# Two MoE stages of a graph network: weight pieces and slots ahead of a branch, two tiles mixed by products, and a shared expert's weights in another ring

## The chip, the cores and the metric

One core of a Trainium2 chip runs the whole kernel. The metric is the device time of one execution in microseconds (us); the time before is the median of three runs. One more execution was taken by the profiler: TensorE (PE) does the matmuls, PEld its weight loads, DVE is VectorE, ACT ScalarE, POOL GpSimd and SP SyncE, whose queue issues the weight transfers. Times in the text are us from the start of the profiled span.

## The reference

256 tokens of width 768 pass through four rounds; each round is a graph layer (gnn) and a feed-forward layer (ffn), with layer norms between, and every ffn adds its output to x. The change concerns the ffn of rounds 1 and 2, both a mixture of eight experts (MoE) of which each token takes two. Cut to what matters, with `x` the normed tokens:

```
# round 1 (layer 1)
logits = x @ Wr.T;  vals, idx = top_k(logits, 2);  weights = softmax(vals)
h = gelu(x @ Wi[e].T + bi[e]);  expert_out[e] = h @ Wo[e].T + bo[e]
out[t] = sum over the token's 2 experts of weights * expert_out[e][t]

# round 2 (layer 2)
w, idx = gate(x)                       # softmax scores, best 2 of 4 groups, best 2 experts
g = swiglu((x @ W1[e] + B1[e]) * (x @ W3[e] + B3[e]));  per_expert[e] = g @ W2[e] + B2[e]
out[t] = sum over 2 experts of w * per_expert[e][t]  +  shared_ffn(x)
shared_ffn(x) = swiglu((x @ Ws1 + Bs1) * (x @ Ws3 + Bs3)) @ Ws2 + Bs2
```

The kernel must be right for any routing; for the input timed here no expert gets more tokens than its tiles hold.

## The kernel before, in words

**Tiles of tokens.** Experts are ranked by their number of tokens (`ranked`, DVE; `who[r]` is the expert of rank r, L1021). Fixed tiles of 128 rows are given to ranks: `TILES1` has seven tiles (rank 0 has one and a half, ranks 1 to 4 one each, 5, 6 and 7 half ones), `TILES2` six. `dispatch` (L1024) works out for each token the two rows it has among all tiles (`places`) and a flag `over`, whether some expert overflows its tiles. If it does, a body under `tc.If(count > 0)` (L1439 and L1667) computes extra tiles; for this input it is jumped over. Every engine reads the flag and takes the branch for itself, and on the way around the body the engines step through semaphores so that all agree on the counts. `find` makes `slots`, the token of each tile row: DVE compares a count with `places` (`hot`, L1099), PE multiplies it with token numbers (L1104), DVE copies the result (L1107).

**A tile's work.** The first tile's rows in layer 1 are picked by products (`first_rows`, L1144). For the other tiles POOL gathers rows from a table in DRAM by indirect DMA (`take_rows`, L1120), PE transposes them (L1128), and PE multiplies: `up` (L1153, after a bias product at L1421 or L1641), then an activation (ACT, and DVE in layer 2), transposes of the result (L1202), and `finish`, the products ps_y with the second weights (L1153 too), ACT's copy to `y` (L1161) and ACT's DMA of `y` into `ys` in DRAM (L1210). The loop over tiles is staggered: up(u), then the transposes and ps_y of tile u - 1.

**Weights.** A piece is 1152 KB. `stream` keeps a list of pieces with their rings; `pump` issues each next one on SP as long as its ring has a free buffer, and `done` frees buffers in program order. Layer 1 has 16 pieces (wi and wo of eight ranks) in the ring "w" (`wpool`, RING = 8 buffers). In layer 2 the w_e pieces go there too, with four of the buffers held at first by the shared expert's up weights (s0 to s3), while w_down pieces and the shared expert's Ws2 go through the ring "d" of three. SP reads `who` into a register to form a piece's address (L1214), then issues the DMA (L87).

**The end of a layer.** Weights of the mix come from `rest` (L1058). It also makes, for the last tile, a mix matrix (`mix`, called neg in the profile, L1071 and L1073; transposed at L1076 and copied by ACT at L1078 to `mixT`), so that this tile's rows never go through DRAM: `end_tiles` multiplies `mixT` with its `y` (L1176) into the accumulators of each half of the tokens, which in layer 1 begin with the bias bo (L1478) and in layer 2 with the shared expert's products (`down_t`, L1114 and L1116). All other rows come back by `add_rows`: four indirect gathers yg from `ys` on POOL (L1120), each multiplied and added to x on DVE (L1169). Then DVE adds the accumulator (`add_acc`, L1370), norms (L150 to L160), and PE's transposes (L171) begin the next stage. Rows of `ys` that are asked for with a weight of zero were zeroed in the first stage.

**Order around the change.** Instructions marked `pin` keep program order on PE; a scheduler places the rest by its own cost estimates. In layer 1 the order before is: `dispatch`, `first_rows`, branch, first `pump`, `find`, softmax, loop. In layer 2: `up_shared(0)` (shared expert, L102), `dispatch`, `up_shared(1)`, branch, `pump`, `find`, first gather, `up_shared(2)`, `rest`, loop.

Of the kernel before, what the change touches and what calls it, by code (L numbers as in the profile page):

```python
# [13 lines left out]
OP = mybir.AluOpType  # L14
# [4 lines left out]
P = 128  # L19
# [34 lines left out]
def graph_ffn_stack_kernel(ctx: ExitStack, tc: tile.TileContext, a: dict, out: bass.AP):  # L54
# [969 lines left out]
    def dispatch(pool, plan_t, mask, before, total, is_r):  # L1024
# [32 lines left out]

        def rest(cw, last):  # L1058


            weights = tmp([P, NC, 2], "row_w")
            for i, t in enumerate((lo, hi)):
                nc.vector.tensor_tensor(t, t, ends[:, :, i, None].to_broadcast([P, NC, 8]), OP.is_equal)
                nc.vector.tensor_tensor(t, t, cw, OP.mult)
                nc.vector.tensor_reduce(weights[:, :, i], t, AX.X, OP.add)
            rel = tmp([P, NC, 2], "row_rel")
            nc.vector.tensor_scalar(rel, places, float(last * P), None, op0=OP.subtract)
            mix = neg1.rearrange("p c (j n) -> p c j n", j=2)
            for c in range(NC):
                for j in range(2):  # L1070
                    nc.vector.tensor_scalar(mix[:, c, j, :], count_up[:, :P], rel[:, c, j:j + 1], weights[:, c, j:j + 1],  # L1071
                                            op0=OP.is_equal, op1=OP.mult)
            nc.vector.tensor_tensor(mix[:, :, 0, :], mix[:, :, 0, :], mix[:, :, 1, :], OP.add)  # L1073
            ps = bank("ps_mix")[:, :N]
            for c in range(NC):
                nc.tensor.transpose(ps[:, c * P:(c + 1) * P], mix[:, c, 0, :], ident)  # L1076
            mixT = cnt1[:, 0, :]
            nc.scalar.copy(mixT, ps)  # L1078
            kept = tmp([P, NC, 2], "row_kept")
            nc.vector.tensor_scalar(kept, rel, 0.0, None, op0=OP.is_lt)  # L1080
            nc.vector.scalar_tensor_tensor(kept, rel, float(P), kept, op0=OP.is_ge, op1=OP.add)
# [81 lines left out]
    def add_rows(gathered, ys, rows, weights):  # L1163
        table = ys.rearrange("u p d -> (u p) d")
        for c in range(NC):
            for j in range(2):
                y = gathered("yg")
                take_rows(y, table, rows[:, c, j:j + 1])
                nc.vector.scalar_tensor_tensor(x[:, c, :], y, weights[:, c, j:j + 1], x[:, c, :], op0=OP.mult, op1=OP.add)  # L1169

    def end_tiles(accs, y, mixT):

        xn = normed()
        for c in range(NC):
            for i in range(2):
                pin(nc.tensor.matmul(accs[c][:, i, :384], mixT[:, c * P:(c + 1) * P], y[:, i * 384:(i + 1) * 384],  # L1176
                                     start=False, stop=True))
            add_acc(accs[c], c)
            norm(x, xn, D, c)
        return xn  # L1180
# [35 lines left out]
    def stream(pieces, held_by_others):  # L1216


        loaded, freed, rings, at = {}, set(), {"w": [None] * (RING - len(held_by_others)) + held_by_others}, [0]
        freed.add(None)  # L1220

        def pump():
            while at[0] < len(pieces):
                key, ring, bufs, load = pieces[at[0]]
                keys = rings.setdefault(ring, [])
                if len(keys) >= bufs and keys[len(keys) - bufs] not in freed:
                    return
                loaded[key] = load()
                keys.append(key)
                at[0] += 1  # L1230

        def done(*keys):
            freed.update(keys)
            pump()

        return loaded, pump, done

    TILES1 = [[(0, 0, 128)], [(0, 128, 64), (7, 0, 64)], *[[(r, 0, 128)] for r in range(1, 5)], [(5, 0, 64), (6, 0, 64)]]
    TILES2 = [[(0, 0, 128)], [(0, 128, 64), (7, 0, 64)], [(1, 0, 128)], [(3, 0, 64), (4, 0, 64)], [(2, 0, 128)],
              [(5, 0, 64), (6, 0, 64)]]  # L1240
    plans = [moe.tile([P, 3, 8], F32, name=f"plan{i}") for i in range(2)]
    results = [held.tile([len(t) + len(plan(t)[3]), P, D], F32, name=f"ys{i}") for i, t in enumerate((TILES1, TILES2))]
# [7 lines left out]
    def constants(pool):  # L1250
        zero = pool.tile([P, D], F32, name="zero")
        nc.gpsimd.memset(zero, 0.0)
        for i, tiles in enumerate((TILES1, TILES2)):
            more = results[i][len(tiles) - 1:]
            nc.gpsimd.dma_start(more.rearrange("u p d -> p u d"), zero[:, None, :].to_broadcast([P, more.shape[0], D]))
            for j, values in enumerate(plan(tiles)[:3]):
                for r, value in enumerate(values):
                    if r == 0 or value != values[r - 1]:
                        nc.gpsimd.memset(plans[i][:, j, r:], float(value))
# [123 lines left out]
    with tc.tile_pool(name="f1", bufs=1) as f1, tc.tile_pool(name="f1a", bufs=2) as f1a:  # L1383
# [10 lines left out]

        def load(r, kind):
            if kind == "wi":
                index[r] = nth(who, r)
            return load_piece(wpool, a["L1_ffn_WiT" if kind == "wi" else "L1_ffn_WoT"][index[r]], kind)

        index = {}  # L1400
        loaded, pump, done = stream([((r, kind), "w", RING, lambda r=r, kind=kind: load(r, kind)) for parts in TILES1
                                     for kind in ("wi", "wo") for r, first, _ in parts if first == 0], [])
        places, is_e, over, rest = dispatch(f1, plans[0], mask, before, total, is_r)
        more = plan(TILES1)[3]
# [31 lines left out]

        xgT = first_rows(f1, places, "first_xgT")
        count = nc.values_load(over[0:1, 0:1], min_val=0, max_val=1, **UNCHECKED)
        with tc.If(count > 0, preferred_fallthrough_block=False):  # L1439
            slots = find(f1, places, len(TILES1) * P, len(more), "slots1_more")  # L1440
            for j, r in enumerate(more):
                parts = [(r, 0, P)]
                for kind in ("wi", "wo"):
                    loaded[r, kind] = load(r, kind)
                g = up(tile_t(f1a, take(slots[:, j:j + 1]), "xgT"), parts, pick(f1a, is_e, parts))
                finish(f1a, ys[len(TILES1) + j], turned(f1a, g), views(parts, "wo"), parts)
            index.clear()
        pump()
        slots = find(f1, places, P, len(TILES1) - 1, "slots1")
        softmax8(cw)  # L1450
# [5 lines left out]
        for u, parts in enumerate(TILES1):  # L1456
            now = xgT
            if u < end:
                xg = take(slots[:, u:u + 1])
            if u == 0:  # L1460
                rows1, w1s, mixT = rest(cw, end)
            g = up(now, parts, pick(f1a, is_e, parts))
            free(u, "wi")
            if last is not None:
                gT = turned(f1a, last)
            if u < end:
                xgT = tile_t(f1a, xg, "xgT")
            if last is not None:
                finish(f1a, ys[u - 1], gT, views(TILES1[u - 1], "wo"), TILES1[u - 1])
                free(u - 1, "wo")  # L1470
            last = g
        add_rows(gathered, ys, rows1, w1s)
        gT = turned(f1a, last)
        accs = []
        for c in range(NC):
            accs.append(acc2("moe_acc"))
            for i in range(2):
                pin(nc.tensor.matmul(accs[c][:, i, :384], cwT[:, c * P:(c + 1) * P], bo[:, i * 384:(i + 1) * 384],  # L1478
                                     start=True, stop=False))
        xn = end_tiles(accs, finish(f1a, None, gT, views(parts, "wo"), parts), mixT)  # L1480

# [52 lines left out]
    with tc.tile_pool(name="f2", bufs=1) as f2, tc.tile_pool(name="f2a", bufs=2) as f2a:  # L1534
# [50 lines left out]
        before, total, is_r, who = ranked(f2, mask)  # L1585
        places, is_e, over, rest = dispatch(f2, plans[1], mask, before, total, is_r)
        index = {}

        def load(r, kind, ring=None):

            if r == "s":
                return load_piece(f2a, a["L2_ffn_Ws2"], "w_down", "down", DOWN)
            if r not in index:
# [97 lines left out]
        rows2, w2s, mixT = rest(cw, end)  # L1691
        cwT = weights_t(f2, cw, 9, "cwT2")
        xgT = tile_t(f2a, xg, "xgT")
        last = None
        for u, parts in enumerate(TILES2):
            own, now = pick(f2a, is_e, parts), xgT
            if u < end:
                xg = take(slots[:, u + 1:u + 2])
            acc = acc2("up1_acc")
# [21 lines left out]
        xn = end_tiles(accs, finish(f2a, None, gT, views(parts, "2"), parts), mixT)  # L1721

# [196 lines left out]
```

## Time and profile before

| what | us |
|---|---|
| median of 3 runs (1452.01 to 1456.68) | 1454.04 |
| the profiled execution | 1456.74 |
| its span in the profile | 1455.0 |
| layer 1's MoE, from the first L1144 product to the next stage's transposes (852.1 to 957.6) | 105.5 |
| layer 2's MoE, from its up_shared(1) to the next stage's transposes (1076.4 to 1257.9) | 181.5 |

The mean granted clock of TensorE over the span is 0.916. The profiled execution is 2.70 us above the median, so a sum made on its rows stands on a time that is that much longer. In the views of groups and waits, "idle before" is the time in which an engine had nothing to do ahead of an instruction, with what released it behind the arrow; a row of the timeline gives the start, the duration, the engine and line, and the tiles written and read. A window's row gives each engine's busy time, the granted clock, the share of the DMA engines and GB/s. Issue and landing of single DMAs, quoted in the text, are from the trace's instruction rows.

### The profile page before, as it was taken

How to read it: one execution, taken by the hardware profiler on the slowest of the kernel's cores; microseconds unless marked ns; L12 is line 12 of the kernel's file. 1: busy time of each engine (PE TensorE's matmuls, PEld its weight loads, DVE VectorE, ACT ScalarE, POOL GpSimd, SP SyncE). 2: the span in 40 equal slices, each digit the busy share in tenths (PEclk: the TensorE clock that was granted, in tenths of full speed). 3: DMA queues.
4: the chain of work that ended last, by engine and by line, in shares of the span. 5: the costliest groups of instructions: out<-in, count | busy, mean ns of one | idle time of the engine just before them, and what ended most of it. 6: DMA issues, size and time to landing. Idle time of an engine off the chain costs nothing. (4 is left out here: it accounts for less than half of the span.)

```text
span 1455.0 us, 13968 instructions
## 1 busy us (share of the span) xinstructions
PE 1259.4 (87%) x5081; PEld 775.6 (53%) x5102; DVE 670.2 (46%) x1273; ACT 477.0 (33%) x825; POOL 356.3 (24%) x194
## 2 busy tenths in 40 slices
PE   7999999789997874998989859866889999777998
PEld 4576444347643432854545445435576554466854
DVE  4421999930099996164352530067351011455023
ACT  1013877611287662241231122215221111163122
POOL 1001999800099991000203010111001000100000
PEclk9999999989999995999999969987989999775989
DMA  9323250215230023223732149922018998600000
GB/s 332 130 94 102 59 160 6 98 33 195 101 95 0 3 95 115 89 111 143 259 116 76 66 171 389 335 89 73 22 72 342 364 383 334 264 1 33 33 0 22
DMA packets 77689, 196.74 MB, mean 135 GB/s; under 512 B 9036, under 2 KB 23952, under 8 KB 77488
## 3 DMA queue, kind: packets, MB, share of 16 engines
q1 hardware_dynamic: 69088, 162.28, 31.2%
q0 software_dynamic: 6352, 28.33, 5.5%
q10 hardware_dynamic: 2176, 5.18, 1.0%
q8 instruction: 43, 0.70, 0.2%
q14 instruction: 30, 0.25, 0.1%
HBM read 177.45 MB, written 14.87 MB: 132 GB/s over the span
## 5 line engine op out<-in xcount | busy, mean ns | idle before, releaser
L784 POOL TENSOR_TENSOR gate<-gate,qT 128x2048 f32<-128x2048 f32 x64 | 287.8, 4535 | 242.4 <-ACT gate L764 242.0
L769 DVE TENSOR_REDUCE qiT<-gate 128x32 f32<-128x2048 f32 x96 | 215.0, 2279 | 16.2 <-POOL gate L784 15.2
L764 ACT ACTIVATE gate<-gate_acc,bg 128x1024 f32<-128x1024 f32 x192 | 209.8, 1114 | 38.1 <-PE gate_acc L760 35.5
L759 PE MATMUL gate_acc<-sela,ga 128*128 128x512 bf16 x363 | 139.2, 384 | 25.3 <-ACT gate L764 24.8
L760 PE MATMUL gate_acc<-selb,gb 112*128 112x512 bf16 x384 | 147.8, 385 | 1.2
L1153 PE MATMUL up_acc<-w_e,xgT 128*64 128x384 f32 (+1 forms) x432 | 96.4, 489 | 0.0
L760 PEld LDWEIGHTS <-gb 112*128 112x128 bf16 x384 | 37.6, 98 | 96.4 <-issue 71.5
L791 DVE TENSOR_TENSOR gate<-gate,ps_qy 128x2048 f32<-128x2048 f32 x32 | 72.9, 2278 | 0.2 <-ACT gate L764 0.2
L1153 PEld LDWEIGHTS up_acc<-w_e,xgT 128*64 128x64 f32 (+1 forms) x432 | 46.9, 154 | 44.7 <-issue 27.3
L759 PEld LDWEIGHTS <-ga 128*128 128x128 bf16 x384 | 37.8, 98 | 47.8 <-issue 2.2
L642 PE MATMUL ps_alpha<-w_qb,qiT 128*128 128x384 f32 x96 | 44.1, 553 | 19.8 <-DVE qiT L769 19.8
L566 DVE TENSOR_TENSOR ps_hg<-ps_hg,hg 128x384 f32<-128x384 f32 x8 | 4.5, 563 | 107.9 <-ACT hg L565 107.9
L326 PE MATMUL ps_pt<-ident,gat_z 128*128 128x128 f32 x104 | 23.8, 366 | 33.6 <-DVE gat_s L318 33.5
L1120 POOL DMA_INDIRECT yg<-ys,rows x8 | 7.6, 953 | 177.3 <-DMA w_a<-in_L_ffn_AT 118.6
L171 PE MATMUL ps_tr<-ident,xn 128*128 128x128 f32 x84 | 17.7, 380 | 35.4 <-DVE xn L160 20.3
L267 DVE CUSTOM_DVE_ANT_0 gat_dot<-xl,row 128x128 f32<-128x128 f32 (+2 forms) x56 | 23.8, 425 | 52.8 <-ACT xl L1520 19.6
L457 PE MATMUL ps_z<-w_rel,xT 128*128 128x384 f32 x144 | 47.9, 486 | 0.0
L457 PE MATMUL ps_z<-w_rel,nT 128*128 128x384 f32 x144 | 47.7, 491 | 0.0
L461 ACT COPY z<-ps_z 128x384 f32<-128x384 f32 x24 | 11.5, 479 | 105.0 <-PE ps_z L457 105.0
L1651 DVE TENSOR_TENSOR h<-up_acc,h 128x768 f32<-128x768 f32 x6 | 5.7, 958 | 80.1 <-PE up_acc L1153 80.1
L627 PE MATMUL ps_alpha<-w_qa,gT 128*128 128x384 f32 x96 | 40.1, 499 | 0.0
L338 PE MATMUL gat_acc<-xl,gat_pt 128*128 128x128 f32 (+2 forms) x128 | 34.9, 431 | 5.3 <-DVE gat_s L347 5.3
(444 smaller groups left out, 2192.7 us busy)
## 6 DMA issues: line engine op xcount, KB each, us to landing
w_e<-in_L_ffn_W SPq DMA_DIRECT2D x32, 1152.0 KB, 12.2
w_rel<-in_L_gnn_W_rel SPq DMA_DIRECT2D x12, 1152.0 KB, 8.3
wi<-in_L_ffn_WiT SPq DMA_DIRECT2D x8, 1152.0 KB, 15.0
wo<-in_L_ffn_WoT SPq DMA_DIRECT2D x8, 1152.0 KB, 15.5
w_down<-in_L_ffn_W SPq DMA_DIRECT2D x8, 1152.0 KB, 12.2
w_root<-in_L_gnn_W_root SPq DMA_DIRECT2D x4, 1152.0 KB, 11.1
w_ga<-in_L_gnn_WgAT SPq DMA_DIRECT2D x4, 1152.0 KB, 6.4
w_qa<-in_L_gnn_WqAT SPq DMA_DIRECT2D x4, 1152.0 KB, 5.7
```

Of the source, the lines that this page charges most:

```text
L267: pin(nc.vector.tensor_tensor_reduce(t, xl[:, c, h * C:(h + 1) * C], r[:, h * C:(h + 1) * C], 1.0, 0.0, OP.mult, OP.add, accum_out=a2[:, w ...
L338: pin(nc.tensor.matmul(accs[d][:, i, at:at + wide], pts[h, d][:, j, s, :], xl[:, s, lo:lo + wide], start=s == 0, stop=s == NC - 1))
L457: mm = nc.tensor.matmul(ps, hT[:, k, c * P:(c + 1) * P], w(k, i * 384, (i + 1) * 384), start=k == 0, stop=k == KD - 1)
L627: pin(nc.tensor.matmul(al_ps[c][i], hT[:, k, c * P:(c + 1) * P], w(k, i * 384, (i + 1) * 384), start=k == 0, stop=False))
L642: pin(nc.tensor.matmul(al_ps[c][i], qiT[:, f, c * P:(c + 1) * P], w(f, i * 384, (i + 1) * 384), start=False, stop=f == KD - 1))
L759: pin(nc.tensor.matmul(acc[:, i, :], ga[:, b, fs], sela, start=True, stop=False))
L760: pin(nc.tensor.matmul(acc[:, i, :], gb[0:112, u, b, fs], selb[0:112, i], start=False, stop=True))
L764: pin(nc.scalar.activation(g[:, u * 16:(u + 1) * 16, :].rearrange("p n l -> p (n l)"), acc.rearrange("p a n -> p (a n)"), AF.Sigmoid, bias ...
L769: pin(nc.vector.tensor_reduce(qiT[:, f, b * NPB:(b + 1) * NPB], g, AX.X, OP.add))
L784: pin(nc.gpsimd.tensor_tensor(g, g, q[:, None, :].to_broadcast([P, NPB, LQ]), OP.mult))
L791: pin(nc.vector.tensor_tensor(g, g, q_ps[:, None, :].to_broadcast([P, NPB, LQ]), OP.mult))
L1153: pin(nc.tensor.matmul(ps[at:at + n, :], xT[:, k, at:at + n], ws[r](k, lo, hi), start=start, stop=stop))
```

## The change

Four things are changed, in the ffn of rounds 1 and 2.

1. `pump` takes a bound, and `pump(4)` is called ahead of `dispatch` in both layers, so that four pieces are issued before the branch. In layer 1 the body of the branch loads its own pieces into a ring of the pool `f1a` instead of `wpool`, and `ahead` keeps the pieces that were issued in front.
2. `find` for the tiles' slots stands ahead of the branch in both layers.
3. `rest` makes mix matrices for the last `n` tiles: two in layer 1, one in layer 2 (as before). In layer 1 tile 5 is no longer written to `ys`; its `y` is multiplied with `mixT[0]` into the accumulators before the last tile's ps_y, and `add_rows` moves into the loop, to u = 6. One more tile of `ys` is zeroed at the start.
4. The shared expert's Ws2 takes a buffer of the ring "w" instead of "d".

```diff
-        def rest(cw, last):
+        def rest(cw, first, n):
...
-            nc.vector.tensor_scalar(rel, places, float(last * P), None, op0=OP.subtract)
+            nc.vector.tensor_scalar(rel, places, float(first * P), None, op0=OP.subtract)
...
+            mixT = [cnt1[:, u, :] for u in range(n)]
+            for u in range(n):
+                for c in range(NC):
+                    for j in range(2):
+                        nc.vector.tensor_scalar(mix[:, c, j, :], count_up[:, u * P:(u + 1) * P], rel[:, c, j:j + 1],
+                                                weights[:, c, j:j + 1], op0=OP.is_equal, op1=OP.mult)
+                nc.vector.tensor_tensor(mix[:, :, 0, :], mix[:, :, 0, :], mix[:, :, 1, :], OP.add)
+                ps = bank("ps_mix")[:, :N]
+                for c in range(NC):
+                    nc.tensor.transpose(ps[:, c * P:(c + 1) * P], mix[:, c, 0, :], ident)
+                nc.scalar.copy(mixT[u], ps)
...
+    def mix_in(acc, y, mixT, c, stop=False):
+        for i in range(2):
+            pin(nc.tensor.matmul(acc[:, i, :384], mixT[:, c * P:(c + 1) * P], y[:, i * 384:(i + 1) * 384],
+                                 start=False, stop=stop))
...
-        def pump():
-            while at[0] < len(pieces):
+        def pump(upto=None):
+            while at[0] < len(pieces if upto is None else pieces[:upto]):
...
+    MIXED = (2, 1)
...
-            more = results[i][len(tiles) - 1:]
+            more = results[i][len(tiles) - MIXED[i]:]
...

+        pump(4)
         places, is_e, over, rest = dispatch(f1, plans[0], mask, before, total, is_r)
...
         xgT = first_rows(f1, places, "first_xgT")
+        slots1 = find(f1, places, P, len(TILES1) - 1, "slots1")
         count = nc.values_load(over[0:1, 0:1], min_val=0, max_val=1, **UNCHECKED)
+        ahead = dict(loaded)
         with tc.If(count > 0, preferred_fallthrough_block=False):
...
-                    loaded[r, kind] = load(r, kind)
+                    loaded[r, kind] = load(r, kind, f1a, "more", 2)
...
+        loaded.update(ahead)
         pump()
-        slots = find(f1, places, P, len(TILES1) - 1, "slots1")
...
-                rows1, w1s, mixT = rest(cw, end)
+                rows1, w1s, mixT = rest(cw, end - 1, 2)
             g = up(now, parts, pick(f1a, is_e, parts))
             free(u, "wi")
+            if u == end:
+                add_rows(gathered, ys, rows1, w1s)
...
-                finish(f1a, ys[u - 1], gT, views(TILES1[u - 1], "wo"), TILES1[u - 1])
+                y = finish(f1a, ys[u - 1] if u < end else None, gT, views(TILES1[u - 1], "wo"), TILES1[u - 1])
...
-        add_rows(gathered, ys, rows1, w1s)
...
-        xn = end_tiles(accs, finish(f1a, None, gT, views(parts, "wo"), parts), mixT)
+        for c in range(NC):
+            mix_in(accs[c], y, mixT[0], c)
+        xn = end_tiles(accs, finish(f1a, None, gT, views(parts, "wo"), parts), mixT[1])
...

-        places, is_e, over, rest = dispatch(f2, plans[1], mask, before, total, is_r)
...
             if r == "s":
-                return load_piece(f2a, a["L2_ffn_Ws2"], "w_down", "down", DOWN)
+                return load_piece(wpool, a["L2_ffn_Ws2"], "w_s2")
...
-        pieces.append((("s", "2"), "d", DOWN, lambda: load("s", "2")))
+        pieces.append((("s", "2"), "w", RING, lambda: load("s", "2")))
         loaded, pump, done = stream(pieces, ["s0", "s1", "s2", "s3"])
+        pump(4)
+        places, is_e, over, rest = dispatch(f2, plans[1], mask, before, total, is_r)
...
         up_shared(1)
+        slots2 = find(f2, places, 0, len(TILES2), "slots2")
         count = nc.values_load(over[0:1, 0:1], min_val=0, max_val=1, **UNCHECKED)
+        ahead = dict(loaded)
...
+        loaded.update(ahead)
         pump()
-        slots = find(f2, places, 0, len(TILES2), "slots2")
-        xg = take(slots[:, 0:1])
+        xg = take(slots2[:, 0:1])
```

The names slots1 and slots2 are used in the loops in place of slots; the rest of the program is the same.

More of the change, by code (lines that the diff above doesn't have):

```diff
@@ L1066, in rest @@
             rel = tmp([P, NC, 2], "row_rel")
-            nc.vector.tensor_scalar(rel, places, float(last * P), None, op0=OP.subtract)
+            nc.vector.tensor_scalar(rel, places, float(first * P), None, op0=OP.subtract)
             mix = neg1.rearrange("p c (j n) -> p c j n", j=2)
[L1069 to L1078, printed above, removed]
+            mixT = [cnt1[:, u, :] for u in range(n)]
[9 more added lines that the diff above has]
+                nc.scalar.copy(mixT[u], ps)
             kept = tmp([P, NC, 2], "row_kept")
             nc.vector.tensor_scalar(kept, rel, 0.0, None, op0=OP.is_lt)
-            nc.vector.scalar_tensor_tensor(kept, rel, float(P), kept, op0=OP.is_ge, op1=OP.add)
+            nc.vector.scalar_tensor_tensor(kept, rel, float(n * P), kept, op0=OP.is_ge, op1=OP.add)
             nc.vector.tensor_tensor(weights, weights, kept, OP.mult)
@@ L1174, in end_tiles @@
         for c in range(NC):
-            for i in range(2):
-                pin(nc.tensor.matmul(accs[c][:, i, :384], mixT[:, c * P:(c + 1) * P], y[:, i * 384:(i + 1) * 384],
-                                     start=False, stop=True))
+            mix_in(accs[c], y, mixT, c, True)
             add_acc(accs[c], c)
@@ L1393, in graph_ffn_stack_kernel, with load @@
         before, total, is_r, who = ranked(f1, mask)
-        def load(r, kind):
+        def load(r, kind, pool=wpool, *ring):
             if kind == "wi":
                 index[r] = nth(who, r)
-            return load_piece(wpool, a["L1_ffn_WiT" if kind == "wi" else "L1_ffn_WoT"][index[r]], kind)
+            return load_piece(pool, a["L1_ffn_WiT" if kind == "wi" else "L1_ffn_WoT"][index[r]], kind, *ring)
         index = {}
@@ L1458, in graph_ffn_stack_kernel @@
             if u < end:
-                xg = take(slots[:, u:u + 1])
+                xg = take(slots1[:, u:u + 1])
             if u == 0:
-                rows1, w1s, mixT = rest(cw, end)
+                rows1, w1s, mixT = rest(cw, end - 1, 2)
             g = up(now, parts, pick(f1a, is_e, parts))
             free(u, "wi")
+            if u == end:
+                add_rows(gathered, ys, rows1, w1s)
             if last is not None:
@@ L1690, in graph_ffn_stack_kernel @@
         end = len(TILES2) - 1
-        rows2, w2s, mixT = rest(cw, end)
+        rows2, w2s, mixT = rest(cw, end, 1)
         cwT = weights_t(f2, cw, 9, "cwT2")
@@ L1697, in graph_ffn_stack_kernel @@
             if u < end:
-                xg = take(slots[:, u + 1:u + 2])
+                xg = take(slots2[:, u + 1:u + 2])
             acc = acc2("up1_acc")
@@ L1720, in graph_ffn_stack_kernel @@
                 gT = turned(f2a, last)
-        xn = end_tiles(accs, finish(f2a, None, gT, views(parts, "2"), parts), mixT)
+        xn = end_tiles(accs, finish(f2a, None, gT, views(parts, "2"), parts), mixT[0])
     with tc.tile_pool(name="g3", bufs=1) as g3, tc.tile_pool(name="g3a", bufs=2) as g3a:
```

## The prediction

> **What bounds the kernel now.** First the busy shares of the page: PE is the bound, the others have air.
>
> ```profile
> PE 1259.4 (87%) x5081; PEld 775.6 (53%) x5102; DVE 670.2 (46%) x1273; ACT 477.0 (33%) x825; POOL 356.3 (24%) x194
> ```
>
> The change touches only the two MoE stages, so I split them into stretches: PE, PEld, DVE, ACT and POOL busy, granted clock, DMA share, GB/s.
>
> ```profile
> 849.00:864.00 15.00, 6.15 (x54) 5.71 (x55) 7.71 (x48) 2.61 (x4) 3.81 (x4) 0.73 0.43 146
> 864.00:883.00 19.00, 15.33 (x54) 7.53 (x54) 0.22 (x1) 3.94 (x8) 1.17 (x3) 0.78 1.03 374
> 883.00:939.00 56.00, 55.43 (x233) 31.20 (x233) 0.74 (x4) 14.29 (x33) 0.84 (x1) 1.00 1.01 368
> 939.00:961.00 22.00, 6.91 (x27) 4.35 (x24) 9.36 (x16) 4.32 (x8) 8.59 (x11) 0.69 0.51 189
> 1081.00:1109.00 28.00, 20.90 (x114) 17.52 (x113) 9.29 (x44) 3.77 (x9) 4.45 (x5) 0.88 0.83 317
> 1109.00:1234.00 125.00, 123.56 (x582) 63.06 (x580) 15.97 (x35) 17.94 (x36) 1.43 (x2) 1.00 0.91 349
> ```
>
> Between the seams PE is full at clock 1.00 (55.43 of 56, 123.56 of 125); nothing is to be had there. The time lies at the seams, where PE is idle and its clock drops. What follows each seam waits for PE, so a seam that shrinks moves all behind it. Four seams, each with its PE, DVE or SP rows of the timeline (start, duration; idle before in brackets):
>
> ```profile
> 856.64 0.41 SPq L87 DMA_DIRECT2D wi<-in_L_ffn_WiT  x1
> ...
> 863.67 6.71 PE L1153 MATMUL up_acc<-wi,first_xgT 128*128 128x384 f32 x12 [4.70 <-DMA wi<-in_L_ffn_WiT]
> ...
> 875.73 5.75 PE L1153 MATMUL up_acc<-wi,xgT 128*64 128x384 f32 x22 [2.20 <-DMA wi<-in_L_ffn_WiT]
> ```
>
> Seam 1, layer 1's start: who is on which rank is known at 849.06 (who, L1021), yet the first weight leaves only at 856.64, after PE has reached its branch (its semaphore step, 856.56). PE waits 4.70 for it, works at half speed (0.64 us from one product to the next against 0.33 later; the same 12 products take 4.03 in tile 2), then waits 2.20 for the next.
>
> ```profile
> 939.65 2.88 PE L1176 MATMUL moe_acc<-y,cnt 128*128 128x384 f32 x8
> 957.62 2.82 PE L171 MATMUL ps_tr<-ident,xn 128*128 128x128 f32 x12 [15.09 <-DVE xn L160]
> ...
> 948.14 1.02 DVE L1169 SCALAR_TENSOR_TENSOR x<-yg,row_w,x 128x768 f32<-128x768 f32 x1 [42.67 <-DMA yg<-ys,rows]
> 950.92 0.96 DVE L1370 TENSOR_TENSOR x<-moe_acc,x 128x768 f32<-128x768 f32 x1
> ```
>
> Seam 2, its end: tile 5 is written at 933.14, landed 939.83, gathered back from 940.74, added from 948.14. PE waits 15.09 for that round trip.
>
> ```profile
> 1093.81 0.78 PE L1104 MATMUL ps_slot<-token,hot 128*128 128x1 bf16 x24 [6.83 <-issue]
> 1094.45 12.15 PE L102 MATMUL ps_e<-xT,w_s 128*128 128x256 f32 x48
> ...
> 1234.93 2.17 PE L1114 MATMUL moe_acc<-w_down,gs 128*128 128x384 f32 x6 [2.36 <-DMA w_down<-in_L_ffn_Ws]
> 1251.08 2.85 PE L1176 MATMUL moe_acc<-y,cnt 128*128 128x384 f32 x8
> 1257.86 2.71 PE L171 MATMUL ps_tr<-ident,xn 128*128 128x128 f32 x12 [3.92 <-DVE xn L160]
> ```
>
> Seam 3, layer 2's start: PE idles 6.83 while DVE passes its branch (1090.0) and makes hot (1.41) for the slots. Seam 4, its end: 2.36 for the shared expert's last weights, issued at 1228.58.
>
> **Part 1, pieces and slots ahead of the branch, layer 1.** (What stands ahead of what in the changed kernel is read from its built instruction order.) After who at 849.06, SP loads the register and issues in some 0.9 us (L1214's 0.28, register steps): first piece about 850, the others to 852. The first landed 7.0 after its issue here and 5.6 in layer 2 (1085.09 to 1090.70): 856 to 857. PE now does first_xgT (to 856.5), the 24 slot products (0.78), its branch and ps_cw (1.0 from 856.56 to 857.57 now): 858.9. It then waits for the second mix matrix, which is new: two more neg (0.27 each by L1071's 1.10 for four) and the add (0.43) on DVE, after its branch and PE's read of the first; I put that at 860.8, so up(0) at 861.3 instead of 863.67. It ends at 865.3 (4.03 warm) to 868.0 (6.71 cold). up(1) needs its gathered rows: the gather still leaves after the branch, about 859, and took 7.05 (859.27 to 866.32), plus transposes and copy, 867.9; or up(0)'s end plus the 2.3 that lies there now. up(1) starts at 867.9 to 870.3 with its weights there, takes 4.1 to 6.6, and with 1.1 for transposes ps_y(0) starts at 873.1 to 878.0 instead of 882.53: gain 4.5 to 9.4. I take **7.0**, the middle.
>
> The price: this adds a wait. On the path around the branch SP steps through the semaphores of all earlier DMAs (nine steps, 851.05 to 851.62, at no cost now, as nothing is in flight). With four pieces in flight it stands there until all have landed, and behind it are pieces 5 to 8. By layer 2's row four pieces landed 16.1 after the first issue (1101.18), by layer 1's 23.0 (879.64, four gathers among them): SP is free at 866 to 873, piece 5 (wi of rank 1) leaves 1.4 later and lands 5.6 to 7.0 after: 873 to 881. up(2) needs it 4.14 after ps_y(0) starts, at 877.2 to 882.1. Likely covered, with 1 to 4 us to spare; the bounds cross at 4 us.
>
> The gathers here split the channel with the pieces: the second piece landed 7.7 after the first, in layer 2 only 4.1. [...]
>
> **Part 2, two tiles by products.** Added on PE: four calls, eight passes, one more L1176 row of 2.88. It lies between L1478 and ps_y(6), on the path, since y(5) is copied by then. Removed: ys(5)'s write and the wait for it. The yg gathers now need only ys(4), landed 929.95, so they leave at about 930.0 in old times; from first gather to last add is 13.45 now (940.74 to 954.19), so the adds end at 943.5. add_acc(0) can start after the first half of the shifted L1176, 942.53 + 1.44 = 944.0. So nothing but add_acc, norm and transposes remains, as in layer 2's end: 1251.08 to 1257.86, 6.78. New: 942.53 + 6.78 = 949.3 against 957.62, gain **8.3**. The slack of DVE is only 0.5; were the gathers as late as now the part would cost 2.88. Each us beyond the slack costs one. The extra zeros for ys, written by POOL in the first stage, lie beside its work; uncovered, 393 KB at 374 GB/s is 1.1.
>
> **Part 3, layer 2's start.** hot goes to DVE right after places (1081.8), so the slots are ready before up_shared(1) ends on PE at 1087.0. Then 0.78, the branch (1.0 by layer 1's row), and up_shared(2) starts at about 1088.8, instead of 1094.45: 5.65. Without the idle its 48 products should take the 10.61 of up_shared(1) instead of 12.15: 1.54. Together 7.2 at most; at least 0, if DVE's own branch still holds what PE reads. The first xg leaves about 1088.5, lands 7.4 later (1095.59 to 1103.00 now), needed at 1100. The four pieces land by 1080.4 + 16.1 = 1096.5, needed at 1101; SP's wait then delays the next ones to 1097, where ring slots held them until 1100.16 anyway. I take **6.5**.
>
> [...]
>
> **Part 4, Ws2.** In the big ring it takes a slot that layer 2's w_e set free, an estimated 12 us earlier; by w_down's median 12.2 from issue to landing it is there before 1232.6. Gain the 2.36 of seam 4, take **2.4**; then yg's adds (end 1249.07) against add_acc at 1250.3 have 1.2 left. The next stage's w_a, w_qk and w_v come one slot later; PE needs none of them up to 1325. If it comes as late as now, 0.
>
> **Sum.** 7.0 + 8.3 + 6.5 + 2.4 = 24.2. The profiled execution took 1456.74 (span 1455.0), 2.70 above the median 1454.04. Against it: 1432.5; against the median: 1429.8. I take the middle, **1431**.
>
> **Rivals.** (a) SP's wait shows: piece 5 lands at 881 where up(2) could start at 877; 4 us of wait, then a cold tile (6.71 - 4.03 = 2.7). 6.7 of the 7.0 are gone: 1438. For it: the 23.0 row and DMA share 1.03. Against: no gathers in the first 9 us now. (b) One of the other two large terms fails: the adds end late, or layer 2's PE waits for DVE's branch. About 6 to 8 lost: 1438. For it: 0.5 slack. Both (a) and (b): 1445. (c) Slower than before: behind SP's wait the pieces never get ahead again, each tile of layer 1 waits and runs at half speed. 9.15 a tile becomes 18.3, five tiles cost 46: 1477. It ends above 1454 from three such tiles on (27.5). For it: 883:939 has DMA share 1.01, so no spare. Against: two pieces take 6 to 7 us of the channel (landings 3.0 to 4.1 apart from 882.77) and a tile 9.15; pieces landed 3.8 us ahead of use and more. (d) The branch's steps are no cover and SP's early issue brings no early landing: parts 1 and 3 bring under 2, 1443.
>
> **Chances.** Forecast 0.60, (a) or (b) 0.24, both or (d) 0.09, (c) 0.04, else 0.03. With all bounds at their good end (9.4, 8.3, 7.2, 2.4) 27.3 is gained: 1427 from the median; I set low 1424 for what I can't see, and high 1444, with (d) in and (c) out. 0.3% is 4.4 us, about what a measurement here can tell from no change. Faster 0.92, within 0.03, slower 0.05.
>
> **What would show it.** Right: first wi issued near 850, up(0) near 861, no DMA idle before up(1); a gap in SP's issues of 14 to 21 us; PE idle before L171 about 4 at layer 1's end; slots on PE before its branch; no idle before L1114. Wrong: an idle before up(2) on DMA wi, clock below 1 beyond 883, or DVE yg rows after L1176's end.

## The result and the profile after

The changed kernel takes 1437.37 us, the median of four runs (1433.95 to 1438.38); the kernel before, 1454.42 beside it. The ratio is 0.9879, 95% interval [0.9855, 0.9903]. So 17.05 us are gone where the sum had 24.2, and the time is 6.4 above the forecast of 1431. The profiled execution took 1433.95 (span 1432.0), the fastest of the four, and that of before 1456.74, a little above all four of its runs (1452.01 to 1456.68); the two traces are 23.0 apart, 6 of which is the choice of runs.

The first rows that answer to those of before are the windows of the changed kernel's stages (busy time of PE, PEld, DVE, ACT and POOL, granted clock, DMA share, GB/s).

```profile
860.00:873.00 13.00, 11.53 (x54) 6.43 (x54) 0.45 (x2) 3.53 (x7) 3.00 (x4) 0.88 0.91 334
873.00:929.00 56.00, 55.43 (x223) 31.54 (x221) 1.06 (x5) 14.56 (x34) 4.78 (x5) 1.00 1.03 380
929.00:942.00 13.00, 9.29 (x44) 5.23 (x44) 9.30 (x16) 3.83 (x8) 5.16 (x7) 0.85 0.81 300
1063.00:1095.00 32.00, 24.66 (x131) 21.19 (x131) 12.71 (x69) 3.39 (x9) 3.93 (x4) 0.89 0.75 281
1095.00:1219.00 124.00, 124.00 (x586) 63.78 (x586) 15.70 (x35) 18.74 (x38) 1.96 (x2) 1.00 0.94 364
```

Layer 1's start and end have become short; 1063:1095, layer 2's start, has still 7.3 us of idle PE. PE's timeline of the changed kernel has the seams in their order:

```profile
860.56 5.30 PE L1154 MATMUL up_acc<-wi,first_xgT 128*128 128x384 f32 x12
868.15 4.09 PE L1154 MATMUL up_acc<-wi,xgT 128*64 128x384 f32 x24 [1.47 <-ACT xgT L1130]
...
926.38 2.85 PE L1174 MATMUL moe_acc<-y,cnt 128*128 128x384 f32 x8
933.18 2.88 PE L1174 MATMUL moe_acc<-y,cnt 128*128 128x384 f32 x8
939.76 2.82 PE L171 MATMUL ps_tr<-ident,xn 128*128 128x128 f32 x12 [3.71 <-DVE xn L160]
...
1042.60 1.54 PE L171 MATMUL ps_tr<-ident,xn 128*128 128x128 f32 x6 [3.06 <-DVE xn L160]
...
1073.47 0.74 PE L1105 MATMUL ps_slot<-token,hot 128*128 128x1 bf16 x24
1081.28 12.42 PE L102 MATMUL ps_e<-xT,w_s 128*128 128x256 f32 x48 [7.07 <-issue]
...
1219.59 2.20 PE L1115 MATMUL moe_acc<-w_s,gs 128*128 128x384 f32 x6
```

No wait for a wi is left in layer 1. Its end waits 3.71 instead of 15.09. L1115 starts without idle. But up_shared(2) still waits 7.07, and its slots, which were to be what it waited for, are done at 1074.2. The wait's releaser is "issue": nothing the profile knows as an instruction's input. The row of before that the prediction passed over stands among the rows of its branch, line L1667, and the same row stands at L1682 now; the columns are minimum, median and maximum in ns, first and last start:

```profile
L1667 PEldq COMPARE_BRANCH  x2: 64/3268/6472, 1083.9 to 1087.2; - x2
```

```profile
L1682 PEldq COMPARE_BRANCH  x2: 64/3126/6188, 1074.7 to 1074.9; - x2
```

PE's sequencer makes two steps at the branch, the compare (64 ns) and the jump around the body. The jump alone takes 6.47 us before and 6.19 after. I had taken that row for a wait.

To see where the 23.0 come from, the same PE instruction is looked up in both traces, and its start after is taken from its start before:

| PE instruction | before | after | gained up to here | gained since the row above | prediction |
|---|---|---|---|---|---|
| first product of first_xgT | 852.10 | 849.68 | 2.4 | 2.4 | 0 |
| ps_y of layer 1's tile 0 | 882.53 | 873.29 | 9.2 | 6.8 | 7.0 |
| transposes after layer 1 | 957.62 | 939.76 | 17.9 | 8.6 | 8.3 |
| up_shared(1) | 1076.37 | 1063.02 | 13.4 | -4.5 | 0 |
| up_shared(2) | 1094.45 | 1081.28 | 13.2 | -0.2 | 6.5 with the row below |
| last up of layer 2 | 1228.47 | 1215.56 | 12.9 | -0.3 | |
| first shared down product | 1234.93 | 1219.59 | 15.3 | 2.4 | 2.4 |
| ps_a of round 3 | 1266.59 | 1249.30 | 17.3 | 2.0 | 0 |
| end of the span | 1455.0 | 1432.0 | 23.0 | 5.7 | 0 |

Three of the four terms are there to within 0.3. One is missing, and amounts stand where nothing was forecast: a loss of 4.5 between the end of layer 1 and up_shared(1) (round 2's graph layer, the router and up_shared(0)), and gains of 2.0 at round 3's start and 5.7 in it. The 2.4 of the first row lies ahead of the products that the change moves; in the fourteen traces of this case that start lies anywhere from 848.28 to 853.81, so it is within what the traces scatter by.

### The profile page after: what moved, and what is told of

The parts are those of the page before. It is cut to its first block, busy times and chain, and to the rows that moved or that the text cites. A ratio compares the mean times of both kernels' runs of the same rounds, so it can differ in the third digit from the quotient of the medians.

```text
span 1432.0 us, 13994 instructions
## 1 busy us (share of the span) xinstructions
PE 1254.5 (88%) x5091; PEld 772.6 (54%) x5112; DVE 672.1 (47%) x1278; ACT 477.0 (33%) x826; POOL 357.1 (25%) x194
## 5 line engine op out<-in xcount | busy, mean ns | idle before, releaser
L326 PE MATMUL ps_pt<-ident,gat_z 128*128 128x128 f32 x104 | 23.4, 362 | 30.8 <-DVE gat_s L318 30.8
L267 DVE CUSTOM_DVE_ANT_0 gat_dot<-xl,row 128x128 f32<-128x128 f32 (+2 forms) x56 | 23.8, 425 | 51.5 <-ACT xl L1532 18.9
L102 PE MATMUL ps_e<-xT,w_s 128*128 128x256 f32 x144 | 36.3, 418 | 7.1 <-issue 7.1
## 6 DMA issues: line engine op xcount, KB each, us to landing
wo<-in_L_ffn_WoT SPq DMA_DIRECT2D x8, 1152.0 KB, 12.9
```

Of the source, the lines that this page charges most:

```text
L102: mm = nc.tensor.matmul(ps, w(k, lo, lo + P), xT[:, k, :], start=start and k == 0, stop=stop and k == kcs - 1)
L267: pin(nc.vector.tensor_tensor_reduce(t, xl[:, c, h * C:(h + 1) * C], r[:, h * C:(h + 1) * C], 1.0, 0.0, OP.mult, OP.add, accum_out=a2[:, w ...
```

## The experiments

**Theory A**: layer 2's start waits for PE's jump, which has to have instructions loaded because the body it passes is long. **Theory B**: PE waits for something else there, DVE's branch, the landings of weights or a bank of the memory that its products go to. Twelve kernels were run. Where one kernel's median is set against another's, each was measured against the kernel before on its own chip; the kernel before had medians of 1453.88 to 1455.28 in these batches.

**e1, a short body.** Edit to the changed kernel; six of the seven extra tiles, which this input doesn't need, are left out:

```diff
-            slots = find(f2, places, len(TILES2) * P, len(more), "slots2_more")
-            for j, r in enumerate(more):
+            slots = find(f2, places, len(TILES2) * P, 1, "slots2_more")
+            for j, r in enumerate(more[:1]):
```

> The jumped-over body of layer 2's branch computes one extra tile instead of seven (the other six are left out; none is needed for this input). Everything else is the changed kernel. Theory A, the time at layer 2's start is PE's own jump across a long body (6.19 us in the changed kernel, 6.47 before, against 0.43 across layer 1's shorter one): the jump falls to about 0.4, PE's idle before up_shared(2) from 7.07 to about 1.3, and the time by 5.5 to 7 us (1430.5 to 1432). Theory B, PE waits there for something else, such as DVE's branch, the four landings or a bank: the idle stays at 7 and the time at 1437.

Measured: 1427.83, ratio 0.9829 [0.9806, 0.9852]. The branch's row and PE's timeline of this kernel:

```profile
L1682 PEldq COMPARE_BRANCH  x2: 64/126/187, 1075.6 to 1075.9; - x2
```

```profile
1074.42 0.74 PE L1105 MATMUL ps_slot<-token,hot 128*128 128x1 bf16 x24
1076.68 10.63 PE L102 MATMUL ps_e<-xT,w_s 128*128 128x256 f32 x48 [1.52 <-ACTq L1682]
```

The jump takes 0.19, the idle 1.52, and the 48 products 10.63 instead of 12.42 (in the changed kernel up_shared(1)'s 48 take 10.61, at a granted clock of 1.00). The edit shortens the body on every engine, but the row that changed with PE's idle is PE's own; DVE's steps at the branch take 47 and 49 ns in both traces, and PE waits for no landing from there to the end of layer 2 in either. So B has fallen. The order of PE's other instructions is the same. The median fell by 9.5, more than the trace's 7.3 at this place; this trace also has 3.2 less in round 3, where the granted clock was half for a shorter time (see the last section).

**e2, three branches instead of one.** The body is cut into three, three and one tiles, each under its own `tc.If` on the same flag:

```diff
-        with tc.If(count > 0, preferred_fallthrough_block=False):
+        for at in range(0, len(more), 3):
...
+            with tc.If(count > 0, preferred_fallthrough_block=False):
```

> The body of layer 2's branch is cut into three branches on the same flag, of three, three and one extra tiles; nothing is left out. Theory A with the length of one jump as its cause: three jumps of about 0.5 us each with their compares instead of one of 6.19, PE's idle falls from 7.07 to about 2.5 and the time by 4 to 5 us. Theory A with the total distance as its cause (all of the body must be passed by instruction loads either way): the three jumps together still take 5 to 6, no gain. Theory B: idle 7, or a little more for the two additional branches.

Measured: 1446.42, 0.9953 [0.9931, 0.9974]; slower than the change by 9. The three jumps took 3.77, 5.95 and 3.69, and PE's idle rose to 14.9:

```profile
1077.59 0.74 PE L1105 MATMUL ps_slot<-token,hot 128*128 128x1 bf16 x24
1093.22 9.11 PE L102 MATMUL ps_e<-xT,w_s 128*128 128x256 f32 x27 [14.89 <-DMA xg<-table,slots]
```

So no expectation hit: it is not the length of the one jump alone. The last body has one tile, as in e1, where the jump takes 0.19; here, right behind two others, it takes 3.69.

**e3, layer 1's body twice as long.**

```diff
-            for j, r in enumerate(more):
+            for j, r in [*enumerate(more)] * 2:
```

> The jumped-over body of layer 1's branch computes its five extra tiles twice, so that it is twice as long; it isn't run for this input. Theory A: layer 1's jump on PE grows from 0.43 us to several (3 to 6), up(0) starts that much later, and the time rises by 2 to 5 us. Theory B: the jump stays at 0.4 and the time at 1437.

Measured: 1439.61, 0.9883 [0.9863, 0.9904]. The row of layer 1's branch in this kernel, and what follows on PE:

```profile
L1448 PEldq COMPARE_BRANCH  x2: 98/3119/6140, 859.1 to 859.4; - x2
```

```profile
865.71 0.58 PE L1384 MATMUL ps_cw<-ident,router_l 128*8 128x128 f32 x2 [7.06 <-issue]
```

In the changed kernel that jump takes 0.43 (maximum 425 ns) and ps_cw waits 1.34. The body isn't run in either; twice its length makes the jump 14 times as long. Counted from the first product of first_xgT, the trace loses 6.7 at ps_cw against the changed kernel; the median loses only 2.2. Part of the reason stands in the trace: with this edit the scheduler laid out round 2 as in the kernel before (see e6), and from the transposes after layer 1 to up_shared(1) PE takes 118.7, not the 123.3 of the changed kernel.

**e4, layer 2's start undone.** No early pieces, slots behind the branch:

```diff
-        pump(4)
         places, is_e, over, rest = dispatch(f2, plans[1], mask, before, total, is_r)
...
-        slots2 = find(f2, places, 0, len(TILES2), "slots2")
         count = nc.values_load(over[0:1, 0:1], min_val=0, max_val=1, **UNCHECKED)
...
+        slots2 = find(f2, places, 0, len(TILES2), "slots2")
         xg = take(slots2[:, 0:1])
```

> The changed kernel with layer 2's start as it was: no piece is issued ahead of dispatch, and the slots are found behind the branch. By the two traces (up_shared(2) 13.35 us earlier before it and 13.17 behind it) this part gained nothing, so the time stays within 1 us of 1437. If the part did gain what the prediction gave it (6.5) and the trace hides it, the time rises to 1443.

Measured: 1436.06, 0.9869 [0.9844, 0.9893]. Part 3 gains nothing as built, as expected. The jump takes 6.25 here too.

**e5, a prefetch hint.** The compare jumps itself, and a hint for it stands on PE some 14 us ahead:

```diff
+        with tc.issue_after(counted[-1].ins):
+            tc.mark_branch_hint_location("over2", "LikelyTaken", [mybir.EngineType.PE])
         up_shared(1)
...
-        with tc.If(count > 0, preferred_fallthrough_block=False):
+        with tc.If(count > 0, preferred_fallthrough_block=True, label="over2"):
```

> The changed kernel, nothing left out, with two edits at layer 2's branch: the compare itself jumps (the body lies next, the way around it behind), and a prefetch hint for PE's branch stands ahead of up_shared(1), some 11 us before the jump. Theory A, the jump waits for instructions to be loaded: loaded in time, it falls from 6.19 us to under 1, PE's idle before up_shared(2) from 7.07 to about 1.5, and the time by 5 to 7 from 1437, as with the short body (1427.8). If the hinted block is pushed out again before the jump, or isn't loaded: idle 7 and 1437. Theory B, something else: idle 7.

Measured: 1438.16, 0.9874 [0.9847, 0.9901]. The jump fell to 4.38 only, and the 16 KB of instructions came at 1080.8, after the jump's start at 1078.9, not after the hint at 1064.6. The time is the 1437 of a hint that doesn't help, but the jump is neither under 1 nor unchanged; PE's idle is 5.16, and its 48 products take 13.38. The hint had no visible effect where it stood. Whether the shorter jump is due to the hint or to the other arrangement of the blocks was not told apart.

**e6, part 2 alone** (two tiles mixed by products), on the kernel before; its diff is the change's own for `rest`, `mix_in`, `MIXED` and layer 1's end.

> The kernel before with part 2 alone (mix matrices for layer 1's last two tiles). By the trace of the changed kernel the layer's end gives 8.6: 1445.3 if that were all. But in the built order this part alone also makes the scheduler place both chunks' transposes ahead of the router's products in round 2 (idle of 3.06 before the second transposes in the changed kernel, a loss of about 2.8) and shifts the order at the start of round 3's ffn. If the loss is real and lasts: 1448; if round 3's new order gains what the two traces differ by there (about 7): 1441.

Measured: 1450.72, 0.9972 [0.9945, 0.9998]: 4.6 less, not 8.6, and none of the three times that were expected. How much earlier than before a PE instruction starts: -0.8 at ps_y of tile 0, 7.8 at the transposes after layer 1 (8.6 gained there), 1.9 at layer 2's slots, 0.6 at ps_a of round 3, 5.1 at the end. So the loss in round 2 and the gain in round 3 both come with this part. The place of most of the loss, on PE in this kernel:

```profile
1049.44 0.88 PE L171 MATMUL ps_tr<-ident,xn 128*128 128x128 f32 x6 [1.18 <-DVE gat_s L347]
1053.37 1.54 PE L171 MATMUL ps_tr<-ident,xn 128*128 128x128 f32 x6 [3.06 <-DVE xn L160]
1054.71 5.13 PE L209 MATMUL ps_router<-router_w,xT 128*128 128x8 f32 x24
```

Both groups of transposes now stand ahead of the router's products, so PE waits 3.06 for the second half of xn with twelve products that it could do. In the kernel before they stood between, with an idle of 0.16:

```profile
1056.31 2.46 PE L209 MATMUL ps_router<-router_w,xT 128*128 128x8 f32 x12 [0.38 <-ACT xT L172]
1058.92 1.54 PE L171 MATMUL ps_tr<-ident,xn 128*128 128x128 f32 x6 [0.16 <-DVE xn L160]
1060.40 2.73 PE L209 MATMUL ps_router<-router_w,xT 128*128 128x8 f32 x12
```

No line of that code was changed; the scheduler orders it by its estimates. The other traces tie the loss and the gain to the order. Four have the old order in rounds 2 and 3 (before, e3, e7, e8): from the transposes after layer 1 to up_shared(1) PE takes 118.7 to 120.1 there, and from ps_a to the first lg_acc of round 3 135.0 to 136.3. Eight have the new order in both (the changed kernel, e1, e2, e4, e5, e6, e9, e12): 123.3 to 124.5, and 130.2 to 132.3. e3 has part 2 too, so it isn't the mixing itself but the order that comes with it.

**e7 and e8, part 1 in layer 1 alone**, and the same with the four pieces only:

```diff
+        pump(4)
         places, is_e, over, rest = dispatch(f1, plans[0], mask, before, total, is_r)
...
         xgT = first_rows(f1, places, "first_xgT")
+        slots1 = find(f1, places, P, len(TILES1) - 1, "slots1")   # e7 only
```

> The kernel before with part 1 alone, in layer 1 (four pieces and the slots ahead of the branch). By the trace of the changed kernel ps_y of tile 0 starts 6.8 earlier: 1447.1. If the pieces behind SP's wait were late without the other parts: above 1450.

> As the run with layer 1's part 1 alone, but the slots stay behind the branch: only the four pieces go ahead. If the landing of the first weight was all that held PE (own is done at 858.65, then 4.70 of idle): up(0) starts near 859, tile 1 still waits for its gather, and the gain is the same 6 to 7 (1447). If the early slots carry part of it: up(1) is held by the gather some 1 to 3 us longer, and the time is that much above the other's.

Measured: e7 1449.27, 0.9956 [0.9941, 0.9971]; e8 1451.26, 0.9977 [0.9957, 0.9996]. In the traces, from the first product of first_xgT to ps_y(0) takes 30.4 before, 22.8 in e7 and 22.6 in e8. So in the traces the early pieces are the whole gain of this part, and the early slots add nothing to it. In e8 layer 1's jump took 2.25 (0.41 in e7), and even so the stretch is not longer. The medians, 2.0 apart the other way, can't tell, as their intervals overlap; both lie above the 1447 that was expected.

**e9, layer 2's body as a loop.** All seven extra tiles are still computed when the flag is set; their code exists once:

```diff
+            left = f2.tile([P, NC, 2], F32, name="places_left")
+            nc.vector.tensor_scalar(left, places, float(len(TILES2) * P), None, op0=OP.subtract)
-            slots = find(f2, places, len(TILES2) * P, len(more), "slots2_more")
-            for j, r in enumerate(more):
...
+            with tc.For_i(0, len(more), 1) as j:
...
+                nc.vector.tensor_copy(own, is_e[:, bass.ds(j, 1)].to_broadcast([72, P]))
+                xgT = tile_t(f2a, take(find(f2a, left, 0, 1, "slots2_more")), "xgT")
+                nc.vector.tensor_scalar(left, left, float(P), None, op0=OP.subtract)
```

> The changed kernel, with the body of layer 2's branch written as a loop over its seven extra tiles, so that PE's code for it is about a sixth as long; it still computes all of them when needed. Theory A (PE's jump waits for its instructions, and length decides): the jump falls from 6.19 us to below 1, PE's idle before up_shared(2) from 7.07 to about 1.5, the time by 6 to 8 to about 1430, as with the body cut to one tile (1427.8). If short code doesn't suffice without its block being loaded by luck (three short bodies in a row took 3.7 to 5.9 each): idle of 4 or more, and 1434 or above.

Measured: 1429.09, 0.9837 [0.9808, 0.9865]; the jump 0.19, the idle 1.53:

```profile
L1682 PEldq COMPARE_BRANCH  x2: 64/127/190, 1076.7 to 1077.0; - x2
```

```profile
1077.82 10.63 PE L102 MATMUL ps_e<-xT,w_s 128*128 128x256 f32 x48 [1.53 <-ACTq L1682]
```

The six runs fall into two groups, 1424.44 to 1425.71 and 1432.48 to 1434.23, three in each, and the median is the mean of the two nearest. The trace is of the faster group; what the slower one lost isn't shown, so neither is that the jump was short in it.

**e10, the order of the transposes.** In layer 2 the second chunk's transposes are queued behind the router's first products:

```diff
+                    with tc.issue_after(last.ins):
+                        ahead_of(c)        # turn_chunk(xn, xT, KD, c)
```

> The changed kernel, with the transposes of the second chunk in layer 2's beginning queued on PE behind the router's products of the first chunk, as the kernel before had them; nothing left out. If the loss seen between the two traces there (offset 16.85 to 14.04) is the scheduler's new order: PE's idle of 3.06 before the second transposes is filled, and the time falls by 2 to 3 (about 1434.5). If the order is not the cause: within 1 of 1437.

Measured: 1436.03, 0.9877 [0.9855, 0.9898]. The idle before the second transposes falls from 3.06 to 1.10, and against the changed kernel's trace 1.4 come back between ps_row and up_shared(0). Over the longer way from the transposes after layer 1 to up_shared(1) nothing is gained (123.4 and 123.3), as the graph layer in between took longer. The medians differ by 1.3, less than was expected, and four to six runs don't resolve that by themselves.

**e11, both.**

> Both edits, the loop in layer 2's body and the order of the transposes. If they add: 8 to 10 below the changed kernel, 1427 to 1429; otherwise as the better of the two.

Measured: **1425.66** (1425.09 to 1426.76), 0.9804 [0.9784, 0.9825], the best of all, below the change by 11.7 in the median and a little below what was expected. The five runs lie within 1.7 us. From the transposes after layer 1 to up_shared(1) PE takes 121.1, 2.2 less than in e9. On PE:

```profile
1042.93 2.12 PE L216 MATMUL ps_router<-router_w,xT 128*128 128x8 f32 x12 [0.38 <-ACT xT L172]
1045.54 1.54 PE L171 MATMUL ps_tr<-ident,xn 128*128 128x128 f32 x6 [0.49 <-DVE xn L160]
...
1073.62 0.74 PE L1112 MATMUL ps_slot<-token,hot 128*128 128x1 bf16 x24
1075.88 10.63 PE L102 MATMUL ps_e<-xT,w_s 128*128 128x256 f32 x48 [1.52 <-ACTq L1687]
```

**e12, the loop with layer 2's old start** (e4's and e9's edits together).

> The loop in layer 2's body, with layer 2's start as before the change (no piece ahead of dispatch, slots behind the branch). It says what part 3 is worth once the jump is short. If the prediction's 6.5 was right for everything but the jump: slower than the run with the loop alone by 4 to 6, since PE then waits for DVE's branch and hot before the slots. If nothing: the same within 1.5.

Measured: 1432.74, 0.9849 [0.9828, 0.9871], 3.7 above e9, a little short of the 4 to 6. As e9's runs lie in two groups, on both sides of e12's (1430.72 to 1433.83), the medians alone don't settle part 3. The traces do. In e12 PE starts up_shared(2) 5.1 after the end of up_shared(1), for the first 5.0 at half the clock:

```profile
1067.82 10.61 PE L102 MATMUL ps_e<-xT,w_s 128*128 128x256 f32 x48
1083.55 13.06 PE L102 MATMUL ps_e<-xT,w_s 128*128 128x256 f32 x48
```

From up_shared(1)'s first product to up_shared(2)'s end PE takes:

| | long body | body as a loop |
|---|---|---|
| old start (before, e4; e12) | 30.2, 30.8 | 28.8 |
| early pieces and slots (after; e9) | 30.7 | 23.4 |

Either edit alone is worth 0 to 2 in this stretch; together 6.9 against before and 7.3 against the changed kernel.

## Why the prediction was right, and where it was wrong

The time lies in the range, and the direction and three terms are right. It is nearer to the 1438 of rival (b), one large term failing, than to the forecast, and one large term did fail. **Part 1** gave 6.8 for 7.0. SP stood at its branch until 864.8, a little shorter than worked out (866 to 873), and piece 5 landed at 871.4 and was needed at 877.4: 6.1 to spare, so rival (a) did not come. Nor is there a sign that the four pieces lengthened the gathers: the two of the first four whose landing is recorded took 6.07 and 5.69, where those of before took 7.04 to 8.86. The issues of the changed kernel show the gap:

```profile
847.56 0.40 SPq L87 DMA_DIRECT2D wi<-in_L_ffn_WiT  x1
...
849.62 1.27 SPq L87 DMA_DIRECT2D wo<-in_L_ffn_WoT  x1
865.91 0.39 SPq L87 DMA_DIRECT2D wi<-in_L_ffn_WiT  x1
```

What was wrong inside this part is the share of the slots: e8 has the gain without them. Rival (c) is refuted by the clock, 1.00 from 873 on, and (d) by the early landing, the fourth piece at 864.50 instead of 879.64.

**Part 2** gave 8.6 for 8.3 at its place. The last yg add ended at 934.39 and add_acc began at 934.80, 0.41 later; the slack was worked out as 0.5:

```profile
933.37 1.02 DVE L1170 SCALAR_TENSOR_TENSOR x<-yg,row_w,x 128x768 f32<-128x768 f32 x1 [0.43 <-DMA yg<-ys,rows]
934.80 0.96 DVE L1376 TENSOR_TENSOR x<-moe_acc,x 128x768 f32<-128x768 f32 x1 [0.41 <-PE moe_acc L1174]
```

But the part was costed at its place alone. In e6 it took 4.6 off the time, because the scheduler laid out the next stages anew: 5.9 lost up to layer 2's slots, 4.5 won in round 3. e3, with part 2 and the old order, has neither (see e6). Of the loss, 2.9 lie between ps_row and up_shared(0) in e6, and 1.4 come back in e10. How the rest comes about in the graph layer, 1 to 3 us, is open, and so is what in round 3's new order gains.

**Part 3** is the step that failed: "the branch (1.0 by layer 1's row)". PE's idle at the branch was 7.07, 6.19 of it the jump, where layer 1's row has 0.42. The price was taken from the nearest branch instead of this one, whose own row stood in the trace of before with 6.47. Before, DVE's branch and hot ended at 1092.1 and PE's jump at 1093.6; the change removed the first and the second was late in its place, 1.5 us behind it. That was the shape of rival (b), a wait in the place of the one removed, but on PE and not DVE. The other pieces of the term held: with the jump short, the idle is 1.5, the 48 products take 10.63, and the stretch falls from 30.2 before to 23.4 in e9, 6.9 for the 6.5.

**Part 4** gave 2.4 as forecast, with w_s2 landed at 1216.9 for 1219.6; it was not run by itself. What was not counted is 2.0 more at round 3's start: ps_a waited 3.93 instead of 6.02 for `own`, which DVE makes from the bd matrices.

**The sum** thus missed by one term of 6.5, while unforeseen ones, -4.5 and 7.7, are in the traces, and 2.4 of scatter. That the traces' 23.0 comes so near to the 24.2 is luck: these amounts happen to make up for the missing term. The medians' 17.05 against the traces' 23.0 is within what the runs scatter (1433.95 to 1438.38 and 1452.01 to 1456.68).

## What to carry to other kernels

In this case a jump on PE around code that is not run cost 2.3 to 6.6 us when a block of instructions arrived in it, and 0.2 to 0.4 when none did; the other engines' steps at layer 2's branch took 34 to 49 ns in the changed kernel. Look up the branch rows of every engine in the stage itself, and take none from another branch. Keep a rarely taken body short in code, a loop if it can be, before moving work in front of it: here either step alone gave 0 to 2 us. Short code is no guarantee: e2's last body of one tile cost 3.69. A change of one stage's instructions can move a scheduler's order stages later; compare the whole order and not the edited place only.

## What the runs showed of the hardware

Jumps on PE by what they pass: 0.19 to 0.29 (one tile or a loop), 0.32 to 0.43 (layer 1's five short tiles; once, in e8, 2.25), 6.14 (ten such), 6.07 to 6.59 (layer 2's seven; 4.38 in e5's arrangement), and 3.69 to 5.95 for three short ones in a row. During the jump of the changed kernel two blocks of 16 KB arrive on an instruction queue (starts 1076.6 and 1078.6). The row of the DMA queues for the 6.4 us around the jump, with packets, MB and share of the engines:

```profile
q8 instruction: 2, 0.03, 2.2%
```

The records of all fourteen traces have the same pattern. Elsewhere a block comes on this queue about once in 250 instructions of PE (the median in the traces of before and after). In each of the fourteen jumps of over 2 us one or two blocks land, and the jump ends 1.35 to 1.53 us after the last one (2.23 in one case, e2's second); in none of the sixteen jumps of under 0.5 us does a block arrive. A block takes 1.0 to 2.0 us there; what the rest of a long jump goes to isn't shown.

The jumps in which a block landed took 2.3 to 6.6 us. During that of the changed kernel the DMA engines were busy with weights, queue q1 alone taking 90.3% of them in the window of the row above; how long such a jump would be with idle DMA was not tried. Why e2's second jump took 5.95 and its third, across one tile, 3.69, where e1's across one tile took 0.19, isn't shown.

The clock: up_shared(2)'s products took 10.63 after 1.5 us of idle and 12.42 after 7.07, 1.8 more, where 1.54 had been read off before. The length of the idle doesn't decide it: e5 has 13.38 after 5.16. In the traces of before, the changed kernel, e5 and e12 the granted clock is half for 6.83 us each time, from 3.3 to 4.0 us after the idle began. What is lost is about half of the part of this time in which the products run: 3.1, 3.7, 5.6 and 5.0 us, for 1.5, 1.8, 2.8 and 2.4 lost.

Round 3 has the same on a larger scale. From lg_acc to p_acc, code that no edit touches, PE takes 28.9 to 29.0 in ten traces, with the granted clock half for 17.07 us, and 23.8 in the four others (e1, e3, e9, e12), with the clock half for 3.41. So 5 us between two traces can come from there; what decides it isn't known.
